# Graph convolution and mixture of experts on one core: bias row by a product, another order of the first loads and of the first projection

## The chip, the cores and the metric

The kernel runs on one core of a Trainium2 chip. The metric is the device time in microseconds of one execution, the median of three runs. Besides these, one execution was recorded by the hardware profiler; its rows are what the text calls the profile or the trace. TensorE multiplies matrices, VectorE (DVE) and ScalarE (ACT) do elementwise work, GpSimd (POOL) makes constants and starts indirect transfers, SyncE (SP) only starts transfers. SP, ACT and POOL each have a queue of transfers of their own; all of them are carried out by the same 16 transfer engines.

## The reference

The input is x (625 rows of 1024), 20000 edges as src and dst (sorted by dst) with a type of 0 or 1, and the weights. Cut to what matters:

```python
h = layernorm(x)
n = ln_weight * h * rsqrt(mean(h**2) + 1e-6)
out = n @ W_root + conv_bias                     # 1024 -> 286
for r in (0, 1):                                 # mean over the edges of one type
    out += segment_sum(n[src] @ W_rel[r] * (type == r), dst) / max(count, 1)
x = x + h + elu(out) @ wo                        # 286 -> 1024
t = layernorm(x)
shared = mean over 2 of gelu(t @ sW1 + sb1) @ sW2 + sb2
gates = t @ rW + rb                              # 8 experts, the two largest, softmax
moe = sum of weight * (gelu(t @ W1[e] + b1[e]) @ W2[e] + b2[e])
result = x + t + shared + moe
```

## The kernel before

All of it is float32 at the edges of each stage; a float32 product shows as two records per product in the trace. The 625 rows are five blocks of 125.

**Edges as a product.** The sums over edges are not gathered. The kernel counts, for every pair of a source and a destination row and for each type, how many edges there are, and multiplies this count matrix with the projected rows. It holds the edges in 160 columns of 125. `edge_columns` (L664) turns the three integer rows into columns: VectorE converts (L667, L670, L672), TensorE transposes (L677, `p_edge`), ACT and VectorE write the half-precision keys `cols` (L687 to L695). For each group of 4 or 8 columns VectorE builds one-hot matrices (`ohs`, `ohk`; three instructions at L849, L850, L852), and TensorE multiplies them into the counts (`cnt`, L868). `count_out` (L811) unpacks finished counts.

**Normalization and transposes.** `stats(t)` (L753) takes mean and variance of block t on VectorE and subtracts the mean on ACT (L765), giving `h`. `to_columns` (L789) transposes h on TensorE (`p_t`, L795, eight per block); ACT evicts the first four with the layer-norm weight as a scale (L801), VectorE the other four (L798). `scales` (L771) works out the two reciprocal roots.

**Projections.** `project(i)` (L886) multiplies one block by one of the three weight matrices: sixteen records of 286 columns (`p_pr`, L891). Projections 0 to 4 are with W_root and are evicted with their scale and the bias `cb` (L901); 5 to 9 and 10 to 14 are with the two W_rel and are split into three bfloat16 parts (L895 to L899). `aggregate(d, r)` (L904) multiplies counts and parts (`p_agg`), takes the edge count of each row from the last column (`deg`, copied by ACT at L911) and adds the mean (L913 to L915). `elu`, `elu_columns` and `output_proj` (L920 to L966) finish the convolution, store the rows and normalize again (`h2`), and `to_columns` brings h2 into `h2T`.

**Experts.** `gate` (L1078) multiplies with the gate weights, `route` (L1102) finds the two largest, `slots` (L1150) gives each pair of row and expert a place in one of eleven tiles. The first layer of the two shared experts, `shared_in` (L1132, `p_sh`), is placed between these steps, so that TensorE works while VectorE routes. Then eleven tiles of gathered rows go through the experts (L1359, L1417), and the second layer of the shared experts is added last (L1472).

**What sets the order.** The code writes an order by hand: `at(c, f, ...)` says that f comes behind the counts of edge column c (L984 to L1021). In front of the loop stand the steps

```python
warm(24)                  # L975: products of constants, only to keep TensorE at work
behind = edge_columns()
transpose_lnw()
warm(40)
ahead = stats(0)
```

`tc.issue_after(x.ins)` says that an instruction stands behind another one in its engine's order. Within these bounds a planner sets each engine's order at build time: it takes by the code's order what it holds to be ready, so that, for example, a projection can be cut in two with counts between. On the chip, each engine then goes through its list in this order. The first loads are issued by SP in this order: edge types, src, x's block 0, W_root, x's blocks 1, 2 and 3 (one transfer), 4, the two W_rel. ACT's queue issues dst and the layer-norm weight. POOL's queue issues the convolution bias, read 125 times into `cb` (L610), then biases and gate weights. Accumulators in PSUM are taken from two rings, `ps_acc` (three slots in the first half) and `ps_mm` (three).

Of the kernel before, what the change touches and what calls it, by code (L numbers as in the profile page):

```python
# [8 lines left out]
F32 = mybir.dt.float32  # L9
# [3 lines left out]
I16 = mybir.dt.int16  # L13
# [439 lines left out]
def sparse_kernel(  # L453
# [68 lines left out]
    for name, v, eng in (("ety", edge_type, nc.sync), ("dst", dst, nc.scalar), ("src", src, nc.sync)):  # L522
        ti = fbig.tile([EH, 2 * EP], I32, name=f"{name}_i")
        eng.dma_start(ti, v.rearrange("(c p) -> c p", p=2 * EP))
        rows_i[name] = ti
# [5 lines left out]
    nc.scalar.dma_start(lnw, ln_w.rearrange("(k p) -> k p", p=128))  # L531

# [9 lines left out]
    def load_w(r, w):  # L542
        nc.sync.dma_start(wg[:, :, r, :], w.rearrange("(k p) f -> p k f", p=128))

    load_x(0, 1)
    load_w(R, W_root)
    load_x(1, 1)
    load_x(2, 2)
# [61 lines left out]
    nc.gpsimd.dma_start(cb, bcast_rows(conv_bias, TP))  # L610
# [53 lines left out]
    def edge_columns():  # L664
# [7 lines left out]
        nc.vector.tensor_copy(rowf[:, 0], rows_i["src"])  # L672
        p = ps_mm("p_edge")
        pv = p[:EP, : 2 * EC].rearrange("p (a j c) -> p a j c", a=2, j=2)
        for a in (0, 1):
            for j in range(2):
                nc.tensor.transpose(pv[:, a, j, :], rowf[:, a, j * EP : (j + 1) * EP], ident[:EH, :EH])  # L677
        wide = [EP, EH, 2, 2]

        def column(v):  # L680
            return v.rearrange("p (c j) b -> p c j b", j=2)

        def pairs(v):
            return v.rearrange("p j c -> p c j")[:, :, :, None].to_broadcast(wide)

        with tc.issue_after(table.ins):
            nc.scalar.copy(column(cols[:, KW_]), pairs(pv[:, 1]))  # L687

        q = fbig.tile([EP, 3, 2, EH], F32, name="q")
        nc.vector.tensor_scalar(q[:, 0], pv[:, 0], -float(TP // 2), 1.0 / TP, op0=ALU.add, op1=ALU.mult)  # L690
        nc.vector.tensor_scalar(q[:, 1], q[:, 0], ROUND, -ROUND, op0=ALU.add, op1=ALU.add)
        nc.vector.scalar_tensor_tensor(q[:, 2], q[:, 1], -float(TP), pv[:, 0], op0=ALU.mult, op1=ALU.add)
        nc.scalar.copy(column(cols[:, SP_]), pairs(q[:, 2]))

        return nc.vector.tensor_scalar(column(cols[:, VV_].bitcast(I16)), pairs(q[:, 1]), 4096.0, 7168.0,  # L695
                                       op0=ALU.mult, op1=ALU.add)
# [39 lines left out]
    def transpose_lnw():  # L736
        p = ps_mm("p_lnw")
        nc.tensor.transpose(p[:, :KD], lnw, ident[:KD, :KD])
        nc.scalar.copy(lT, p[:, :KD])

# [12 lines left out]
    def stats(t):  # L753
        st = small.tile([TP, 2, 6], F32, tag="st", name=f"st_{t}")
        for s in range(2):
            with tc.issue_after((second[0] if t > 1 else evicted[1] if t else behind).ins):
# [4 lines left out]
        h = rows.tile([TP, D], F32, tag="h", name=f"h_{t}")  # L761
        with ExitStack() as order:
            if t == 1:
                order.enter_context(tc.issue_after(evicted[0].ins))
            moved = nc.scalar.activation(h, xh[:TP, t, :], AF.Identity, bias=neg)  # L765
# [61 lines left out]

    def count_windows(between):
        accs = []
        c0 = 0  # L830
        for g in GROUPS:
            oh_s = oneh.tile([EP, MAXG, 128], F16, tag="oh_s", name=f"ohs_{c0}")
            oh_k = oneh.tile([EP, MAXG, KR], F16, tag="oh_k", name=f"ohk_{c0}")

            def both(what, n):
                return [EP, g, n // 2, 2], cols[:, what, c0 : c0 + g][:, :, None, :].to_broadcast([EP, g, n // 2, 2])

            def halves(v):
                return v.rearrange("p g (a b) -> p g a b", b=2)

            order = ExitStack()
            if c0 == 0:
                order.enter_context(tc.issue_after(ahead.ins))
            elif c0 == 8:
                order.enter_context(tc.issue_after(second[0].ins))
            row = iota[:EP].rearrange("p (a b) -> p a b", b=2)
            shape, key = both(SP_, 128)
            os = halves(oh_s[:, :g, :])
            nc.vector.tensor_tensor(os, row[:, None].to_broadcast(shape), key, op=ALU.is_equal)  # L849
            nc.vector.tensor_tensor(os, os, both(VV_, 128)[1], op=ALU.mult)  # L850
            shape, key = both(KW_, KR)
            nc.vector.tensor_tensor(halves(oh_k[:, :g, :]), row[:, None, :SPAN].to_broadcast(shape), key,  # L852
                                    op=ALU.is_equal)
            order.close()
# [49 lines left out]
    def aggregate(d, r):  # L904
# [6 lines left out]
        nc.scalar.copy(deg[:, R * d + r : R * d + r + 1], p[:TP, F : F + 1])  # L911
        inv = small.tile([TP, 2], F32, tag="inv", name=f"inv_{d}_{r}")
        nc.vector.tensor_scalar(inv[:, 0:1], p[:TP, F : F + 1], 1.0, None, op0=ALU.max)  # L913
# [61 lines left out]
    warm(24)  # L975
    behind = edge_columns()
    transpose_lnw()
    warm(40)
    ahead = stats(0)
# [7 lines left out]
    for t, (c0, c1) in enumerate(((0, 3), (4, 9), (13, 19), (16, 22), (20, 26))):  # L987
        if t:
            at(c0, stats, t)
        at(c1, to_columns, t, None, nT, True)  # L990
# [11 lines left out]
    at(6, scales, 0, 2)  # L1002
    at(18, scales, 2, 4)
    at(21, scales, 4, NT)
    for i, c in enumerate((7, 15, 21, 24, 28, 46, 64, 82, 100, 118, 134, 148)):
        at(c, project, i)
# [21 lines left out]

    count_windows(between)
# [13 lines left out]
    load_w1(range(2))  # L1043
    sh_in = ExitStack()
# [478 lines left out]
```

## Time and profile before

| what | value |
|---|---|
| median of three runs | 304.66 us (304.27 to 304.80) |
| the profiled execution, its own time | 303.7 us |
| its span, first to last instruction | 301.4 us |
| instructions | 4682 |
| mean granted TensorE clock | 0.997 |
| read from HBM, written | 42.76 MB, 18.81 MB |
| x's block 0, W_root: last packet ends | 5.61 us, 10.42 us |
| first projection (`p_pr`) starts | 11.79 us |
| first shared product (`p_sh`) starts, rank product starts | 130.04 us, 143.27 us |
| last product ends | 296.2 us |

The profile's rows give, for a group of instructions, the engine, the line, the operation, what it writes and reads, the count, and the time. Times are from the span's start. PEld is the loading of weights, which runs beside the products. In the chain of waits each piece was released by the one before it or stood behind it on its engine; a wait names the engine that waits, the engine it waits for, the total, the number of times and the longest one.

### The profile page before, as it was taken

Reading aid. Unit: us, or ns where it says so; the run is one execution under the profiler, and the core shown is the slowest. Engines: PE = TensorE matmul, PEld = TensorE weight load, DVE = VectorE, ACT = ScalarE, POOL = GpSimd, SP = SyncE. Lnnn points to the kernel's source line nnn. Section 1 sums busy time; section 2 is a strip of 40 time slices with the busy share of each in tenths; the row PEclk is TensorE's granted clock in tenths of the full one; section 3 lists DMA queues with packets and bytes.
Section 4 is the critical chain, followed back from the end, with each engine's and each line's share of the span. In section 5 each row is a group of like instructions: output and inputs, shape, how many; then the busy total and the mean of one; then the engine's idle time right before and its main releaser. Section 6 shows DMA issues by size and latency. Waiting matters only on the chain.

```text
span 301.4 us, 4682 instructions
## 1 busy us (share of the span) xinstructions
PE 290.8 (96%) x1649; PEld 194.9 (65%) x1649; DVE 168.4 (56%) x465; ACT 107.5 (36%) x246; POOL 45.2 (15%) x98
## 2 busy tenths in 40 slices
PE   8799999999999799999999999999999999999993
PEld 6687777787889534376777887887843334444452
DVE  5999999998327668756883122212223211255921
ACT  2455118355334432155123244638359311000000
POOL 9500000000000014240131212210003222200000
PEclk9999999999999999999999999999999999999998
DMA  7999910000009999965999253340057555479442
GB/s 243 304 318 393 421 65 2 0 2 1 0 17 340 348 348 391 400 195 182 348 396 410 86 203 96 114 141 3 0 190 276 221 209 210 191 291 385 161 138 73
DMA packets 27408, 61.15 MB, mean 203 GB/s; under 512 B 2176, under 2 KB 16007, under 8 KB 27375
## 3 DMA queue, kind: packets, MB, share of 16 engines
q1 hardware_dynamic: 21806, 43.77, 40.7%
q0 software_dynamic: 5280, 16.69, 15.7%
q10 hardware_dynamic: 294, 0.35, 0.5%
q8 instruction: 15, 0.25, 0.3%
q14 instruction: 13, 0.10, 0.1%
HBM read 42.76 MB, written 18.81 MB: 204 GB/s over the span
## 4 chain that ended last, share of the span: by engine, by line
PE 93%; DVE 4%; ACT 1%; issue 0%; ACTq 0%
PE p_pr L891 20%; PE p_h L1359 13%; PE p_yj L1417 13%; PE p_o L1472 11%; PE p_sh L1137 10%; PE p_y L952 6%; PE p_agg L909 6%; PE p_x L1340 3%; PE p_t L795 3%; PE cnt L868 2%; PE p_y L956 2%; PE p_hT L1371 1%; PE scrap L972 1%; PE p_gate L1085 1%; PE p_o L1474 1%; DVE ln_4s L727 0%
## 5 line engine op out<-in xcount | busy, mean ns | idle before, releaser
L891 PE MATMUL p_pr<-wg,nT 128*125 128x286 f32 x240 | 62.5, 409 | 0.0
L891 PEld LDWEIGHTS p_pr<-wg,nT 128*125 128x125 f32 x240 | 43.2, 187 | 11.3 <-ACT nT L801 0.2
L1359 PE MATMUL p_h<-w1a,xsT 128*128 (+2 forms) x176 | 40.0, 380 | 0.0
L1417 PE MATMUL p_yj<-w2a,hjT 128*128 (+2 forms) x88 | 38.6, 594 | 0.0
L1472 PE MATMUL p_o<-sw,shT 128*125 128x512 f32 (+1 forms) x88 | 36.1, 553 | 0.0
L1137 PE MATMUL p_sh<-h2T,sw 128*128 128x313 f32 (+1 forms) x128 | 35.2, 428 | 0.0
L1359 PEld LDWEIGHTS p_h<-w1a,xsT 128*128 128x128 f32 (+2 forms) x176 | 28.7, 168 | 7.4 <-issue 0.5
L1137 PEld LDWEIGHTS p_sh<-h2T,sw 128*128 128x128 f32 x128 | 23.6, 189 | 8.6 <-issue 0.2
L1417 PEld LDWEIGHTS p_yj<-w2a,hjT 128*128 128x128 f32 (+2 forms) x88 | 14.4, 168 | 22.4 <-issue 22.4
L1472 PEld LDWEIGHTS p_o<-sw,shT 128*125 128x125 f32 x88 | 16.4, 187 | 16.9 <-issue 16.2
L1421 DVE COPY ys<-p_yj 128x512 f32<-128x512 f32 x15 | 10.4, 692 | 28.7 <-PE p_yj L1417 26.5
L1363 DVE COPY hj<-p_h 128x256 f32<-128x256 f32 x11 | 4.7, 425 | 30.8 <-PE p_h L1359 30.8
L909 PE MATMUL p_agg<-P,CT 125*125 125x287 bf16 x150 | 20.1, 287 | 1.6 <-DVE agg L915 1.6
L966 POOL DMA_DIRECT2D x1d<-xh x10 | 5.3, 532 | 98.5 <-DVE xh L959 98.5
L909 PEld LDWEIGHTS <-CT 125*125 125x125 bf16 x150 | 18.5, 136 | 2.5 <-issue 2.0
L1425 POOL DMA_INDIRECT yt<-ys,row x11 | 10.8, 984 | 50.5 <-DVE ys L1421 50.5
L952 PE MATMUL p_y<-wo_t,eT 128*125 128x512 f32 x40 | 18.1, 595 | 0.0
L1332 POOL DMA_INDIRECT xs<-h2d,tok x11 | 11.2, 1015 | 45.0 <-PE p_x L1340 30.9
L1374 ACT ACTIVATE hjT<-p_hT,vT 128x128 f32<-128x128 f32 (+2 forms) x34 | 8.7, 332 | 24.5 <-PE p_hT L1371 24.5
L1344 DVE COPY xsT<-p_x 128x512 f32<-128x512 f32 x11 | 7.6, 692 | 17.4 <-PE p_x L1340 13.8
L1448 DVE SCALAR_TENSOR_TENSOR x<-p_o,x 125x512 f32<-125x512 f32 (+1 forms) x11 | 6.9, 641 | 16.3 <-PE p_o L1474 16.3
L1359 PE MATMUL p_h<-w1m,xsT 128*64 128x256 f32 (+1 forms) x96 | 14.7, 381 | 0.0
(302 smaller groups left out, 424.0 us busy)
## 6 DMA issues: line engine op xcount, KB each, us to landing
w1a<-in_L_ffn_W_dram SPq DMA_DIRECT2D x8, 1024.0 KB, 10.5
w2a<-in_L_ffn_W_dram SPq DMA_DIRECT2D x8, 1024.0 KB, 4.8
yt<-zero SPq DMA_DIRECT2D x2, 2560.0 KB
g<-yt SPq DMA_DIRECT2D x10, 512.0 KB, 6.7
sw<-in_L_ffn_sW_dram SPq DMA_DIRECT2D x4, 1024.0 KB, 5.0
x<-x1d SPq DMA_DIRECT2D x5, 500.0 KB
wg<-in_L_gnn_W_rel_dram SPq DMA_DIRECT2D x2, 1144.0 KB, 19.1
x1d<-xh POOLq DMA_DIRECT2D x5, 448.0 KB, 6.7
```

The costliest lines, as they stand in the source:

```text
L795: nc.tensor.transpose(pv[:, k, :], row[:, at : at + 128], ident[:TP, :TP])
L891: nc.tensor.matmul(p[:TP, :F], nT[:, k, m * TP : (m + 1) * TP], wg[:, k, r, :], start=(k == 0), stop=(k == KD - 1))
L909: nc.tensor.matmul(p[:TP, : F + 1], CT[:, m, at : at + TP], P[:, m, r, i], start=(m == 0 and i == 0), stop=(m == NT - 1 and i == 2))
L952: nc.tensor.matmul(ps[s][:TP, :], eT[:, k, :], wo_t[:, k, s * 512 : (s + 1) * 512], start=(k == 0), stop=False)
L1137: nc.tensor.matmul(p[:, : z - a], sw1[:, i, k, t * 128 : (t + 1) * 128], h2T[:, k, a:z], start=(k == 0), stop=(k == KD - 1))
L1332: nc.gpsimd.indirect_dma_start(out=xs, out_offset=None, in_=h2d, in_offset=bass.IndirectOffsetOnAxis(ap=tok[:, j : j + 1], axis=0))
L1340: nc.tensor.transpose(p[:, k * 128 : (k + 1) * 128], xs[:, at : at + 128], ident)
L1359: nc.tensor.matmul(p[a:b, :H], xsT[j][:, k, a:b], w1m[j, a][:, 0, k, :] if a else w1a[:, bass.ds(e, 1), k, :], start=(k == 0), stop=(k == ...
L1417: made = nc.tensor.matmul(p[a:b], hjT[:, j, k, a:b], w2m[j, a, k][:, at] if a else w2a[:, bass.ds(e, 1), k, at], start=(k == 0), stop=(k = ...
L1421: nc.vector.tensor_copy(y[:, at], p)
L1425: sent.append(nc.gpsimd.indirect_dma_start(out=yt, out_offset=bass.IndirectOffsetOnAxis(ap=row[:, j : j + 1], axis=0), in_=y, in_offset=No ...
L1472: nc.tensor.matmul(p[:TP, :n], shT[:, i, k, own], sw2[:, i, k, at], start=(i == 0 and k == 0), stop=False)
```

## The change

The convolution bias is loaded as one row by ACT's queue and spread over the 125 rows by a product with a row of ones, in place of the repeated load by POOL's queue. src is issued by ACT's queue. x's block 1 is issued ahead of W_root, and W_root in two halves. The statistics of block 0 stand ahead of the source columns on VectorE, and for blocks 0 and 1 the subtraction of the mean is divided between ACT (384 columns) and VectorE (640). The edge transposes go to two PSUM tiles, and the source keys are written by VectorE alone. The fillers are 18 and 14 in place of 24 and 40. Transposes and projection of block 0 come ahead of all counts; the one-hots of the first four columns are built behind block 0's eviction, and later projections stand some columns earlier. The degrees are copied by VectorE. The first product of the shared experts (sixteen records) is written out ahead of the transposes of the last block, and the other shared products are tied behind the gate's last product and behind the load counts.

```diff
-    for name, v, eng in (("ety", edge_type, nc.sync), ("dst", dst, nc.scalar), ("src", src, nc.sync)):
+    for name, v, eng in (("ety", edge_type, nc.sync), ("dst", dst, nc.scalar), ("src", src, nc.scalar)):
...
+    cb1 = fbig.tile([1, F], F32, name="cb1")
+    nc.scalar.dma_start(cb1, conv_bias.rearrange("(o f) -> o f", o=1))
...
-    def load_w(r, w):
-        nc.sync.dma_start(wg[:, :, r, :], w.rearrange("(k p) f -> p k f", p=128))
+    def load_w(r, w, *ks):
+        for k in ks or (slice(0, KD),):
+            nc.sync.dma_start(wg[:, k, r, :], w.rearrange("(k p) f -> p k f", p=128)[:, k])
     load_x(0, 1)
-    load_w(R, W_root)
     load_x(1, 1)
+    load_w(R, W_root, slice(0, KD // 2), slice(KD // 2, KD))
     load_x(2, 2)
...
     cb = gbig.tile([TP, F], F32, name="cb")
-    nc.gpsimd.dma_start(cb, bcast_rows(conv_bias, TP))
+    one = fbig.tile([1, TP], F32, name="one")
+    nc.vector.memset(one, 1.0)
...
+        ps = [ps_acc("p_edge"), ps_mm("p_edge_k")]
         for a in (0, 1):
             for j in range(2):
-                nc.tensor.transpose(pv[:, a, j, :], rowf[:, a, j * EP : (j + 1) * EP], ident[:EH, :EH])
+                nc.tensor.transpose(ps[a][:EP, j:EC:2], rowf[:, a, j * EP : (j + 1) * EP], ident[:EH, :EH])
...
-        nc.vector.scalar_tensor_tensor(q[:, 2], q[:, 1], -float(TP), pv[:, 0], op0=ALU.mult, op1=ALU.add)
-        nc.scalar.copy(column(cols[:, SP_]), pairs(q[:, 2]))
+        nc.vector.scalar_tensor_tensor(cols[:, SP_], pairs(q[:, 1]), -float(TP), pairs(v),
+                                       op0=ALU.mult, op1=ALU.add)
...
         nc.scalar.copy(lT, p[:, :KD])
+        p = ps_mm("p_cb")
+        nc.tensor.matmul(p[:TP, :F], one, cb1, start=True, stop=True)
+        nc.scalar.copy(cb, p[:TP, :F])
...
-            with tc.issue_after((second[0] if t > 1 else evicted[1] if t else behind).ins):
+            with tc.issue_after((second[0] if t > 1 else first if t else behind).ins):
                 nc.vector.bn_stats(st[:, s, :], xh[:TP, t, s * 512 : (s + 1) * 512])
...
+        own, rest = (slice(0, 384), slice(384, D)) if t < 2 else (slice(0, D), None)
...
-            moved = nc.scalar.activation(h, xh[:TP, t, :], AF.Identity, bias=neg)
+            moved = nc.scalar.activation(h[:, own], xh[:TP, t, own], AF.Identity, bias=neg)
+        if rest:
+            with tc.issue_after(last.ins):
+                last = nc.vector.tensor_scalar(h[:, rest], xh[:TP, t, rest], neg, None, op0=ALU.add)
...
+            if c0 < 8:
+                order.enter_context(tc.issue_after((second[0] if c0 else evicted[1]).ins))
...
-        nc.scalar.copy(deg[:, R * d + r : R * d + r + 1], p[:TP, F : F + 1])
+        n = deg[:, R * d + r : R * d + r + 1]
+        nc.vector.tensor_copy(n, p[:TP, F : F + 1])
         inv = small.tile([TP, 2], F32, tag="inv", name=f"inv_{d}_{r}")
-        nc.vector.tensor_scalar(inv[:, 0:1], p[:TP, F : F + 1], 1.0, None, op0=ALU.max)
+        nc.vector.tensor_scalar(inv[:, 0:1], n, 1.0, None, op0=ALU.max)
...
-    warm(24)
-    behind = edge_columns()
+    warm(18)
+    behind, sources = edge_columns()
     transpose_lnw()
-    warm(40)
-    ahead = stats(0)
+    warm(14)
+    source_columns(sources, stats(0))
+    to_columns(0, hs[0], nT, True)
...
-    for t, (c0, c1) in enumerate(((0, 3), (4, 9), (13, 19), (16, 22), (20, 26))):
+    for t, (c0, c1) in enumerate(((0, 3), (6, 11), (9, 14), (13, 18))):
         if t:
-            at(c0, stats, t)
-        at(c1, to_columns, t, None, nT, True)
+            at(c0, stats, t + 1)
+        at(c1, to_columns, t + 1, None, nT, True)
...
-    at(6, scales, 0, 2)
-    at(18, scales, 2, 4)
-    at(21, scales, 4, NT)
-    for i, c in enumerate((7, 15, 21, 24, 28, 46, 64, 82, 100, 118, 134, 148)):
-        at(c, project, i)
+    at(10, scales, 2, 4)
+    at(14, scales, 4, NT)
+    for i, c in enumerate((3, 12, 15, 20, 38, 56, 74, 92, 110, 128, 146)):
+        at(c, project, i + 1)
...
+    oh_s, oh_k, first = one_hots(0, GROUPS[0])
+    made[0] = oh_s, oh_k
+    stats(1)
+    scales(0, 2)
+    project(0)
     count_windows(between)
...
+        if s == NT + 1:
+
+            p_first = ps_acc("p_sh_first")
+            for k in range(KD):
+                nc.tensor.matmul(p_first[:, : CUTS[0][1]], sw1[:, 0, k, :128], h2T[:, k, : CUTS[0][1]],
+                                 start=(k == 0), stop=(k == KD - 1))
         if 0 <= s - 2 < NT:
             to_columns(s - 2, h2s[s - 2], h2T, False)
...
-        shared_in(0, 0)
+        shared_in(0, 0, gated)
...
-        shared_in(0, 1)
+        shared_in(0, 1, loaded)
```

## The prediction

> **What bounds the kernel now.** I read first the page's busy times and slices, then the chain of waits with the list of what TensorE waits for, then the transfers in half-microsecond windows, then the timeline of the two other places where TensorE stands still.
>
> ```profile
> PE 290.8 (96%) x1649; PEld 194.9 (65%) x1649; DVE 168.4 (56%) x465; ACT 107.5 (36%) x246; POOL 45.2 (15%) x98
> ...
> PE   8799999999999799999999999999999999999993
> ...
> DVE  5999999998327668756883122212223211255921
> ```
>
> TensorE is full from the second slice to the last. VectorE is full too, but only from 7.5 to about 68 us: after that it has room. So time comes only from TensorE's idle places, and VectorE must feed whatever starts earlier.
>
> ```profile
> 5.21 0.88 PE p_edge L677 x4
> ...
> 6.57 0.34 DVE q L690
> ...
> 7.76 1.21 DVE st L757 x2
> ...
> 9.91 0.35 DVE ohs L850
> ...
> 10.62 1.07 PE p_t L795 x8
> 11.70 0.11 PE cnt L868 x4
> 11.81 4.10 PE p_pr L891 x16
> ```
>
> Start, length and work of the chain. What stands before 10.3 us is preparation; the products at L972 are fillers that only keep TensorE busy. From 11.81 on, one piece of product work follows another, so each microsecond by which the first projection (p_pr) starts earlier is a microsecond at the end, if its followers keep up.
>
> ```profile
> PE cnt L868 <- DVE ohs L850: 1.7, 1, 1.7
> PE p_agg L909 <- DVE agg L915: 1.6, 1, 1.6
> ...
> PE p_t L795 <- DVE h L731: 0.6, 1, 0.6
> ```
>
> These are TensorE's waits behind the start: 1.7 (8.6 to 10.3 us), 1.6 (to 100.16) and 0.6 (to 133.47). Nothing else is to be had.
>
> ```profile
> 7.00:7.50 0.50, 0.50 (x12) 0.50 (x10) 0.47 (x3) 0.00 (x0) 0.50 (x2) 1.00 1.91 398
> 7.50:8.00 0.50, 0.50 (x12) 0.50 (x10) 0.50 (x3) 0.44 (x1) 0.48 (x2) 1.00 0.92 121
> 8.00:8.50 0.50, 0.50 (x11) 0.44 (x8) 0.50 (x2) 0.02 (x1) 0.17 (x1) 1.00 1.06 108
> 8.50:9.00 0.50, 0.11 (x3) 0.00 (x0) 0.47 (x2) 0.00 (x0) 0.00 (x0) 1.00 0.53 55
> 9.00:9.50 0.50, 0.00 (x0) 0.00 (x0) 0.47 (x3) 0.08 (x1) 0.00 (x0) 1.00 0.61 206
> ```
>
> The last column is GB/s. Between 7.5 and 9.5 us it falls from about 390 to a mean of 122. The trace's packets tell why: in just this time the bias's 31 broadcast packets of 4576 bytes run at about 0.9 us each, and the packets of W_root, 51 ns each around them, hardly move. W_root's last packet ends at 10.42 us, x's row 0's at 5.61.
>
> **The start, step by step.** *Edge columns.* The fillers ahead fall from 24 to 18. The 24 took 2.74 us, so the edge transposes could start 0.5 us earlier, about 4.5; their last input (the src copy) is ready at 4.22. They end at 5.5. That they go to two banks frees VectorE from waiting for ACT's copy (6.54 today), but it works on row 0 then, so nothing. The memset of ones is 0.06 before any input is there. src moves from SP's queue to ACT's: SP loses 0.41 us of issue ahead of x's row 0, ACT gains 0.41 and, for the bias row, about 0.5; ACT's table load moves from 1.80 to 2.7 and ends at 4.0, before ACT's first copy at 5.5, so nobody sees it.
>
> *Row 0's statistics.* They now stand ahead of the source columns on VectorE, right behind the src copy (4.22), but need x's row 0. Issued 0.46 earlier (1.19 for 1.65), it lands at 5.15, between 4.7 (most of it is there by 4.82 today) and 5.6 (no earlier than today, if src in ACT's queue takes its turns). From 5.15: statistics, mean and negation take 1.65 today (7.76 to 9.39), so 6.8; then h in two parts side by side. VectorE's 640 columns: 1024 take 0.81 at L731 and 286 take 0.30 at L927, so 0.55. ACT's 384 of 1024 (1.15 today): 0.55. h is there at about 7.4, where it is 10.57 today.
>
> *Bias product and fillers.* Two records of 286 columns, 0.5 us on TensorE, and a 0.45 us copy on ACT, at about 6.0 and 6.5: in the wait for h. Then 14 fillers at 0.06 are 0.84, to about 7. The other 18 removed cost nothing. Here the Trainium skill speaks against the change (TensorE: Matmul & The Clock Gate, Part 1): about 3.4 us of sustained work release the full clock. The row: the first 24 fillers take 114 ns each and the later 40 take 60, so the clock comes up between 5.0 and 6.2, with TensorE at work since 1.5. The changed start is as dense up to 7, and today 1.7 us of idling slows nothing (8 transposes in 1.07, as later). By the row the cost is nil; were the release missed, by the rule up to 3.4 us at half speed, 1.7 lost.
>
> *First projection.* Transposes of row 0 from 7.45; today the projection starts 1.17 behind them, so 8.6 in place of 11.79. It no longer waits for the one-hots of the first four edge columns (9.3 to 10.3 today).
>
> *Does W_root arrive?* Row 1 of x (512 KB) now goes ahead of it, 1.4 us at the 375 GB/s of 5 to 7 us. But half of W_root is enough to begin (572 KB, 1.5 us); the second is wanted 2.05 later; the extra issue is 0.43 on SP. Row 0's main part to about 4.4, row 1 to 5.8, first half to 7.4, second to 9; with today's spread between the transfer engines (0.8 for row 0) 8.2 and 9.8, for 8.6 and 10.65. This holds only because the broadcast goes. By the skill's fit (DMA: Bandwidth & Descriptors, Anatomy of one DMA: 2.0 us plus bytes over 436 GB/s) its 143 KB take 0.33 us of bandwidth from others; by the row it is (390 - 122) x 2.0 = 536 KB, 1.4 us. I take the row: by the rule, the second half would still be hit by what the broadcast does. The GpSimd queue behind it (vec, rb, bd, rW) comes 0.8 to 3 us earlier, since bd's 2.3 us wait for the broadcast goes too; the slow stretch at 13.75 to 15 (229 GB/s for 410, some 0.5 us) then falls on x's later rows, which landed 2 us before they were used.
>
> **What follows behind.** VectorE: source columns 1.3 (ACT's 0.46 copy becomes part of one of its four operations) to 8.65; row 0's eviction 0.65 to 9.3; one-hots of the first four columns 0.7 to 10.0; row 1's statistics and h 2.2 to about 12.3. The projection ends at 12.7, so row 1's transposes start at 12.8 and projection 1 at 14.0, in place of 16.89: 2.9, as no counts are left to fill the 0.2 between. VectorE gains 2.6 by starting its long run at 5.1 instead of 7.7, and pays 1.3 for the source columns and 1.1 for two parts of h. It is thus only about 0.2 earlier while TensorE is 2.9 earlier. The counts in the program stand 8 columns (1.75 us of one-hots) later at each projection, so 1 us is missing; today it is ahead by ten to eighteen columns at 37 us, 2 to 4 us. Later TensorE takes counts as they come (counts at 53.68 behind one-hots that end at 53.62), with projections between them, and 15 us of projection and aggregation remain after the last count at 73.1. That cover is shortened by 3 and holds. Front: 3.0 (from 2.5 to 3.5).
>
> **Aggregation.** ACT's degree copy goes (0.16, x10), VectorE's comes (0.15). At the 1.6 us wait, ACT copied late (98.61, behind an exponential) and VectorE stood 0.35 for it. Bounds: 0.5 gained if the copy goes first, 0.1 lost if it stands behind L928. I take 0.2; elsewhere 0.15 lies beside products.
>
> **Shared experts.** Today ten of the sixteen records of the first product fill the gap before row 4's transposes and 0.63 us stays idle; two pairs of records fill the gate's gaps.
>
> ```profile
> 130.04 2.80 PE L1137 MATMUL p_sh<-h2T,sw 128*128 128x313 f32 x10
> 133.47 1.04 PE L795 MATMUL p_t<-ident,h 125*128 125x125 f32 x8 [0.63 <-DVE h L731]
> 134.44 1.92 PE L1085 MATMUL p_gate<-h2T,rw_t 128*32 128x125 f32 x64
> 136.29 0.80 PE L1137 MATMUL p_sh<-h2T,sw 128*128 128x313 f32 x2
> ```
>
> All sixteen (at 0.266: 4.27) now go first, to 134.3, so the transposes start 0.84 later but meet no idle time. The rest waits for the gate's last product. From 130.04 to the rank product at 143.43 are 13.39; work is 32 x 0.266 + 1.00 + 1.84 + 0.56 + 0.44 = 12.36. Left over in future: TensorE behind the gate's second VectorE copy (0.35 and two handovers, less a 0.30 transpose), about 0.2, and 0.15 of changes. Gain 0.7, from 0.3 (the second pair of gaps opens fully) to 0.9. The routing takes VectorE 2.95 from the gate's last product, under the 4.27 of the sixteen records behind it. Tying the next shared product behind the load counts moves nothing: it stands there today.
>
> **Sum.** 3.0 + 0.2 + 0.7 = 3.9. The profiled execution took 303.7 (span 301.4, 2.3 around it), so 299.8; the median is 304.66, 0.96 above it, so 300.8. A difference within 0.2% can't be told from none here.
>
> **Rivals.** *The forecast*, 66%: 299.8 to 301.8. *VectorE takes over in part*, 12%: row 1's h or the later one-hots come about 1.5 late; for it: 98% busy from 10 to 60 us; against: today's lead. 302.3. *Row 1 delays W_root*, 7%: if the slow stretch comes from other small transfers, the first half lands at 10.4 as W_root does today, 1.8 gone: 302.6. *The clock stays down*, 3%: 302.5. *The order isn't what it says*, 5%: if the planner puts the first projection behind the counts again, only the two later parts are left and the time is 303.8 to 304.5. *Slower*, 7%: the last projections stand behind the last count in TensorE's order. If they are held there, TensorE goes at the pace of VectorE's one-hots, which end at 72.1 today. VectorE's run has 2.4 us more in it and pauses for evictions; should row 0 land at 5.6 and two pauses of 1.0 come, the last one-hot is 1.6 late and the whole front with it: 304.66 + 1.6 - 0.9 = 305.4. This decides from the point where the one-hots end more than 0.9 later than now.
>
> Range 299.6 to 303.0: the first four cases but their edges. Faster 0.89, same 0.04, slower 0.07, out of the same cases.
>
> **What would show it.** First projection at 8.6, second near 14.0; the rate at 7.5 to 9.5 us near 380; W_root's halves before 8.6 and 10.6; no count waiting for one-hots between 15 and 73 us; no idle time ahead of row 4's last transposes and the rank product 0.7 closer behind the first shared product. Wrong if the first projection starts at 10 or later, or TensorE shows new waits of over 1 us for one-hots.

## The result and the profile after

The changed kernel takes 306.28 us (median of five runs, 306.10 to 306.96), the kernel before 304.49 us beside it (304.27 to 304.80): a ratio of 1.006, with an interval of 1.0045 to 1.0075. It is slower by 0.6%, clear of the noise, and the forecast was 300.8. The profiled execution of the changed kernel took 306.33 us with a span of 304.1; that of the kernel before 303.7 and 301.4.

TensorE's places in the two traces divide the difference; the forecast's column is worked out from its own terms (its 3.0 in front and 0.2 in the aggregation together move the first `p_y`).

| stretch on TensorE, us | before | forecast | after |
|---|---|---|---|
| start to first projection (`p_pr`) | 11.79 | 8.60 | 11.91 |
| first projection to first `p_y` | 90.85 | 90.85 | 93.17 |
| first `p_y` to first shared product | 27.40 | 27.40 | 27.39 |
| first shared product to rank product | 13.23 | 12.53 | 13.28 |
| rank product to the end of the last product | 152.95 | 152.95 | 152.95 |
| from there to the end of the span | 5.23 | 5.23 | 5.43 |

So 3.3 us are missing at the start, 2.3 up to the first `p_y`, 0.75 in the middle. The timeline of TensorE in the start of the changed kernel (start, length, work; in brackets the idle time ahead and what ended it):

```profile
2.59 2.10 PE L988 MATMUL scrap<-iota 128*128 128x128 f16 x18
6.40 0.68 PE L680 MATMUL p_edge<-ident,rowf 80*125 80x80 f32 x2 [1.71 <-DVE rowf L676]
6.87 0.62 PE L680 MATMUL p_edge_k<-ident,rowf 80*125 80x80 f32 x2
7.42 0.27 PE L741 MATMUL p_lnw<-ident,lnw 8*128 8x8 f32 x1
7.55 1.29 PE L744 MATMUL p_cb<-cb,one 1*125 1x286 f32 x2
8.77 1.67 PE L988 MATMUL scrap<-iota 128*128 128x128 f16 x14
10.24 1.87 PE L806 MATMUL p_t<-ident,h 125*128 125x125 f32 x8
11.91 4.57 PE L906 MATMUL p_pr<-wg,nT 128*125 128x286 f32 x16
```

Two things are to be seen. There is a hole of 1.71 us ahead of the edge transposes. And every row is long: a filler takes 119 ns in the second group too, the transposes 1.87 (1.07 before), the projection 4.57 (4.12 before). In the kernel before the second group ran at 60 ns each:

```profile
6.21 2.41 PE L972 MATMUL scrap<-iota 128*128 128x128 f16 x40
```

In the trace's own clock record the full clock begins at 12.98 us; in the kernel before it began at 6.22. The profile's clock column shows 1.00 for the start in either case, so it can't be used here: the record holds nothing ahead of its first entry, and only the durations show that TensorE ran at half speed until then. h of block 0 is written by 8.53 us; its transposes stand behind slow fillers until 10.24.

The chain of waits begins with the cause of the hole:

```profile
1.20 4.67 DMA src_i<-in_src_dram
```

src, now in ACT's queue, lands at 5.36 us (last packet); in SP's queue, ahead of x's rows, it landed at 3.03. Clock entries and packets are counted here from the span's start, like the instructions. The table of the kernel before, the prediction and the expectations count them from 0.24 us earlier: the table's 5.61 and 10.42 us are 5.37 and 10.18. The list of TensorE's waits has one new entry in the front and two in the middle, and the one at `p_agg` (1.6 before) is where it was:

```profile
PE p_agg L924 <- DVE agg L931: 1.5, 1, 1.5
PE p_gate L1112 <- DVE gT L1115: 0.6, 1, 0.6
PE p_t L806 <- ACT h L773: 0.4, 1, 0.4
PE p_gr L1119 <- DVE gT L1115: 0.2, 1, 0.2
```

What the bias product was meant for did happen. The rate (last column, GB/s) no longer falls at 7.5 us:

```profile
7.50:8.00 0.50, 0.50 (x2) 0.50 (x3) 0.43 (x3) 0.47 (x3) 0.50 (x2) 1.00 1.09 374
8.00:8.50 0.50, 0.50 (x2) 0.02 (x1) 0.50 (x2) 0.50 (x2) 0.50 (x1) 1.00 1.09 349
```

W_root's first half lands at 8.47 us and the second at 10.22, row 0 of x at 5.68 (8.2, 9.8 and 5.15 in the forecast, by its count). The weights were there; the work was not ready for them.

### The profile page after: what moved, and what is told of

The parts are those of the page before. It is cut to its first block, busy times and chain, and to the rows that moved or that the text cites. A ratio compares the mean times of both kernels' runs of the same rounds, so it can differ in the third digit from the quotient of the medians.

```text
span 304.1 us, 4626 instructions
## 1 busy us (share of the span) xinstructions
PE 292.3 (96%) x1619; PEld 194.6 (64%) x1619; DVE 171.1 (56%) x478; ACT 104.9 (35%) x236; POOL 44.5 (15%) x97
## 4 chain that ended last, share of the span: by engine, by line
PE 90%; DVE 5%; DMA 2%; ACT 1%; issue 1%; ACTq 0%; DVEq 0%
PE p_pr L906 17%; PE p_h L1391 13%; PE p_yj L1449 13%; PE p_o L1504 11%; PE p_sh L1169 10%; PE p_y L968 6%; PE p_agg L924 4%; PE p_x L1372 3%; PE p_t L806 3%; PE p_y L972 2%; DMA src_i<-in_src_dram 2%; PE cnt L883 1%; PE p_sh_first L1089 1%; DVE ct L827 1%; PE p_hT L1403 1%; PE p_gate L1112 1%
## 5 line engine op out<-in xcount | busy, mean ns | idle before, releaser
L906 PE MATMUL p_pr<-wg,nT 128*125 128x286 f32 x240 | 64.0, 413 | 0.1
L1169 PE MATMUL p_sh<-h2T,sw 128*128 128x312 f32 (+1 forms) x112 | 30.4, 428 | 0.0
L1169 PEld LDWEIGHTS p_sh<-h2T,sw 128*128 128x128 f32 x112 | 20.9, 189 | 7.7
L1364 POOL DMA_INDIRECT xs<-h2d,tok x11 | 10.6, 961 | 45.8 <-PE p_x L1372 30.9
```

What stands on the lines that cost most here:

```text
L906: nc.tensor.matmul(p[:TP, :F], nT[:, k, m * TP : (m + 1) * TP], wg[:, k, r, :], start=(k == 0), stop=(k == KD - 1))
L1169: nc.tensor.matmul(p[:, : z - a], sw1[:, i, k, t * 128 : (t + 1) * 128], h2T[:, k, a:z], start=(k == 0), stop=(k == KD - 1))
L1364: nc.gpsimd.indirect_dma_start(out=xs, out_offset=None, in_=h2d, in_offset=bass.IndirectOffsetOnAxis(ap=tok[:, j : j + 1], axis=0))
```

## The experiments

Theory A: src's late landing and a late clock hold up the start. Theory B: VectorE has become the bound, and the start hardly matters. Theory C: the middle part takes back what it gives. Times of one batch stand beside runs of the kernel before on the same chip, whose medians were 305.49, 304.98, 304.52 and 304.78 us in the four batches. Single times of one kernel there spread over 2.6 to 3.7 us, so the positions in the traces carry most of the argument. These are the runs, with the time from which the clock record has the full clock:

| run | fillers ahead of the edge transposes | full clock from | fillers behind, ns each | first projection | first `p_y` |
|---|---|---|---|---|---|
| before | 24 | 6.22 | 60 | 11.79 | 102.64 |
| before once more (e8) | 24 | 5.96 | 60 | 11.79 | 103.67 |
| before, src on ACT (e3) | 24, then 0.88 idle | 11.55 | 110 | 12.90 | 103.75 |
| before, bias by product (e4) | 24, then that product | 10.51 | 96 | 12.41 | 103.27 |
| before, 18 fillers (e9) | 18 | 10.57 | 111 | 11.45 | 102.53 |
| after | 18, then 1.71 idle | 12.98 | 119 | 11.91 | 105.08 |
| after, src on SP (e1) | 18 | 10.31 | 120 | 10.37 | 103.33 |
| e1, bias product later (e5) | 18 | 15.50 | 119 | 11.47 | 104.99 |
| after, 34 fillers (e2) | 34 | 6.05 | 68 | 10.14 | 102.85 |
| after, both mended (e6) | 34 | 5.72 | 68 | 9.91 | 102.90 |

**e1: src back in SP's queue.**

```diff
-("src", src, nc.scalar)
+("src", src, nc.sync)
```

> The changed kernel with src issued by SP ahead of x's row 0 again; all else stays. Theory A (the late src is the whole cause): src's last packet ends near 3.3 us instead of 5.6, the edge transposes start at 4.7 instead of 6.4, TensorE has no 1.7 us hole there, its fillers behind run at 60 ns instead of 119, the first projection starts near 9.0 instead of 11.91, the sixth (first with a W_rel) near 35.8 instead of 38.65, and the time is 303.4 or less. Rival B (VectorE's longer list in front of the first projections is a bound of its own): the first projection comes to about 9.0 all the same, but the sixth only to 37 or so, and the time stays at 304 to 305. Rival C (x's row 0, not src, sets the start): the first projection stays above 10.5.

304.72 us, ratio 0.998 [0.996, 1.0001], span 302.4. src lands at 3.00, the edge transposes start at 4.62 and the hole is gone; the first projection comes 1.54 earlier, at 10.37 and not near 9.0 as theory A had it. The fillers stayed slow:

```profile
4.62 0.68 PE L680 MATMUL p_edge<-ident,rowf 80*125 80x80 f32 x2
6.99 1.68 PE L988 MATMUL scrap<-iota 128*128 128x128 f16 x14
```

The clock came only at 10.31, though TensorE had next to no idle time from 1.6 us on (0.03). The late src is a cause, not the only one.

**e2: 34 fillers in front, src left on ACT.**

```diff
-    warm(18)
+    warm(34)
```

> The changed kernel with 34 fillers instead of 18 ahead of the edge transposes, so that TensorE has work until src is there; src stays late. Theory A with the clock as its larger part: the edge transposes start at 6.5 as before the edit, but the bias product takes about 0.5 instead of 1.29, the 14 fillers about 0.85 instead of 1.67, the eight transposes 1.07 instead of 1.87; the first projection starts near 9.8 instead of 11.91 and the time falls by about 2. If the clock played no part and only the late src did: first projection within 0.3 of 11.9, time within 0.5 of the changed kernel's.

304.74 us, ratio 0.9982 [0.9945, 1.0018], span 302.2. This alone brings 1.9 us of span back:

```profile
2.59 3.71 PE L988 MATMUL scrap<-iota 128*128 128x128 f16 x34
6.48 0.41 PE L680 MATMUL p_edge<-ident,rowf 80*125 80x80 f32 x2 [0.18 <-DVE rowf L676]
```

The edge transposes are as late as in the changed kernel, but take 0.41 in place of 0.68, and all that follows is at full speed.

**e3 and e4: one part of the change, put into the kernel before.** e3 moves src to ACT's queue. e4 spreads the bias by the product.

> The kernel before with one edit: src issued by ACT's queue instead of SP's. Theory A: src's last packet ends past 5 us instead of at 3.3, since x's row 0 and W_root fill the same transfer engines from SP's queue; the edge transposes start near 6.0 instead of 4.9, the first projection about 1 later than 11.79, and the time is 0.8 to 1.5 above the kernel before. Rival (the late src comes from something else in the change, such as row 1 of x ahead of W_root): src lands before 4 us and the time is within 0.3 of the kernel before.

> The kernel before with one edit: the bias row spread by a product instead of loaded 125 times. Both theories: the rate between 7.5 and 9.5 us rises from a mean of 122 GB/s to over 300, W_root's last packet ends near 8.8 us instead of 10.42; since the first projection starts at 11.79 for other reasons, the time stays within 0.4 of the kernel before. A gain of 1 us or more would mean that W_root had been a bound.

e3: 305.82 us, ratio 1.0009 [0.9985, 1.0034], span 303.1; src lands at 4.87, the first projection is 1.1 later. e4: 304.79 us, ratio 0.9989 [0.9972, 1.0006], span 302.3; W_root lands at 8.79 for 10.18 and the slump is gone (398 GB/s from 7.5 to 9.5 us for 123), which the first projection does not use, since it waits for VectorE's one-hots; it comes 0.6 later, by the clock. Both parts, harmless in the prediction, delay the clock, by 5.3 and 4.3 us, in a kernel whose fillers were sufficient.

**e5: the bias product behind block 0's transposes** (src on SP), to see whether this product of a single row is what keeps the clock down.

```diff
-        p = ps_mm("p_cb")            # in transpose_lnw
+    spread_bias(to_columns(0, hs[0], nT, True))   # tied behind the last transpose
```

> The changed kernel with src back in SP's queue and the bias product moved behind block 0's eight transposes, where TensorE waits for the evictions. Theory 1 (the bias product, 286 columns of work on a single row, is what keeps the clock down in the start): the clock is full by 6.3 to 7.5 us, fillers behind the edge transposes at 60 ns, the first projection at 8.7 to 9.3 in place of 10.37 with the product in its old place, span 301.0 (302.4 less 1.4). Theory 2 (the time of the release is not set by what TensorE does in this start, it differs from run to run): it comes anywhere between 6 and 13 us, and the first projection with it.

306.32 us, ratio 1.0047 [1.0028, 1.0067], span 304.4. The theory fell: without the product in the start the clock came later still, at 15.50, and the first projection took 6.10 us. What the mended starts have and this one lacks is the longer run of fillers.

**e6, e7: 34 fillers and src on SP; e7 also frees the shared product.**

```diff
-        shared_in(0, 0, gated)
+        shared_in(0, 0)
```

> The changed kernel with src in SP's queue and 34 fillers in front for 18. Theory 1 (unbroken dense fillers release the clock, as with 34 fillers and late src at 6.29): full clock at 6.3, edge transposes at 5.5, first projection at 9.2 to 9.6, span 301.6, about 0.6 less than with late src (302.2), since the fillers themselves now reach to 5.4. Theory 2 (release not set by the work): anything from 6 to 13 us, first projection up to 11. Theory 3 (VectorE sets the later projections): whatever the first projection gains, projection 3 waits again for VectorE's or ACT's h, and the sixth projection starts no earlier than 36.2.

> As the kernel with both mended, but the second half of the first shared product is no longer tied behind the gate's last product, so records of it can fill the gate's gaps. Theory (the tie took as much as the first product ahead of the transposes gave): from the first shared product to the rank product 12.6 to 12.8 us in place of 13.28, the 0.6 us wait of p_gate for gT gone, span 0.5 less than with the tie. Rival (the gaps come from VectorE's chain whatever stands in them): 13.2 or more.

e6: 303.64 us, ratio 0.9979 [0.9948, 1.0009], span 301.6. First projection at 9.91, 1.88 ahead of the kernel before; the first `p_y`, at 102.90, is 2.2 ahead of the changed kernel's and not ahead of the kernel before at all. So theory A explains the start, which does matter, and some 2 us are lost behind it (1.9 in e7). Of the expectation's theories, the first has the clock right and the first projection a little early, and the third fits: the sixth projection starts at 36.48. e7: 304.9 us, ratio 0.9994 [0.9969, 1.0018], span 301.2. Its gate waits are gone, but from the first shared product to the rank product it still takes 13.25. The gap has only moved, as TensorE's line shows, and then VectorE's timeline why:

```profile
143.29 0.23 PE L1189 MATMUL p_rank<-sel,below 125*125 125x40 f16 x1 [0.67 <-DVE sel L1143]
```

```profile
141.76 0.91 DVE L637 MEMSET b2x<- 96x1024 f32 x1 [0.16 <-issue]
142.59 0.42 DVE L1142 TENSOR_REDUCE cnt<-above 125x40 f32<-125x320 f32 x1
143.05 0.18 DVE L1143 TENSOR_SCALAR sel<-cnt 125x40 f16<-125x40 f32 x1
```

A memset of 0.91 us for a later stage stands ahead of `cnt` and `sel` in VectorE's order. In the kernel before it stood behind `sel`:

```profile
141.39 0.18 DVE L1115 TENSOR_SCALAR sel<-cnt 125x40 f16<-125x40 f32 x1
141.73 0.91 DVE L633 MEMSET b2x<- 96x1024 f32 x1 [0.15 <-DVE sel L1115]
```

The planner moved it; no line of the diff mentions it. It stands ahead of `sel` in the changed kernel too, but there the tie has already delayed TensorE, so that `sel` is ready in time.

**e8: the kernel before once more.**

> The kernel before, unchanged, once more. Theory 1 (work sets the release of the clock): full clock at 6.3 to 6.6 us again and the first projection at 11.8. Theory 2 (it differs from run to run): full clock at another time, up to 3 us away; the fillers behind the edge transposes then take over 100 ns.

304.92 us, ratio 1.0001 [0.9978, 1.0025]. The clock and the first projection come again about where they did (5.96 and 11.79). But the first `p_y` is 1.03 later, and the span 303.3 for 301.4. One of VectorE's waits, which the first profile does not have, is about as long:

```profile
DVE st L757 <- DMA xh<-in_x_dram: 0.9, 2, 0.8
```

In this run W_root landed at 11.23 for 10.18, and x's rows behind it came late for the statistics. e12 and e13, with the same loads, show this wait too (2.2 and 0.4); the first profile and e9 do not. So the first profile, from which the forecast was worked out, was a lucky one. In all five the packets of the bias's broadcast end only just ahead of W_root's (9.7 to 10.7 us). That the broadcast is what makes the rows late in some executions is likely, and not shown.

**e9: the kernel before with 18 fillers for 24.**

> The kernel before with 18 fillers ahead of the edge transposes for 24 and nothing else. Theory (the clock's release needs a stretch of about 3.4 us that dense fillers fill; with 18 they end at 4.6 and every such stretch holds the edge transposes or a hole): the clock is not full at 6.5 us but at 9 to 13, the 40 fillers behind take over 100 ns each, the first projection starts at 12.3 to 13.5 in place of 11.79, span 302.3 to 303.5. Rival (the two sorts of start differ for another reason): full clock at 6.3 to 6.6, first projection at 11.8 or up to 0.4 earlier, span 301.0 to 301.5.

304.8 us, ratio 1.0002 [0.9978, 1.0027], span 301.3. The clock came at 10.57, as the theory said, and the first projection at 11.45, which it had not said:

```profile
5.62 4.45 PE L972 MATMUL scrap<-iota 128*128 128x128 f16 x40
9.87 0.40 PE L868 MATMUL cnt<-ohk,ohs 125*128 125x58 f16 x4
```

Forty fillers at 111 ns just fill the wait for the one-hots. In the old order a late clock is hidden by that wait; in the changed order the wait is removed, and with it the cover.

**e10: VectorE's memset tied behind `sel`** (on e7).

```diff
-        nc.vector.memset(b2x, 0.0)
+        with tc.issue_after(chosen.ins):      # chosen: the instruction that writes sel
+            nc.vector.memset(b2x, 0.0)
```

> As the kernel with both mended and the shared product untied, but VectorE's memset of 0.91 us (b2x) is put behind the instruction that writes sel, ahead of which it stands in the changed kernel's order of VectorE (in the kernel before it stands behind). Theory (this memset took what the middle part should give): the wait of p_rank for sel (0.7 us) goes, the first shared product to the rank product takes 12.6 us in place of 13.25, span about 300.6. Rival (the second wait of 0.1 to 0.3 comes from elsewhere, p_load then waits): 12.9 to 13.2.

303.72 us, ratio 0.9974 [0.9951, 0.9996], span 301.0: faster than the kernel before, just clear of the noise. VectorE's order, then TensorE's rank product:

```profile
142.40 0.18 DVE L1144 TENSOR_SCALAR sel<-cnt 125x40 f16<-125x40 f32 x1
142.74 0.91 DVE L638 MEMSET b2x<- 96x1024 f32 x1 [0.15 <-DVE sel L1144]
```

```profile
142.69 0.18 PE L1191 MATMUL p_rank<-sel,below 125*125 125x40 f16 x1
```

From the first shared product (130.28) that is 12.41 us, without a wait: 0.84 less. Theory C holds, in two steps, the tie and the memset.

**e11, e12: less work for VectorE.** The multiplication of the one-hots with their value is left out for all but the first four columns; e11 on e7, e12 on the kernel before. The counts are then wrong, and behind them the kernel takes a far longer way (1254.63 and 1256.96 us in all), so only the part up to the first `p_y` is read.

```diff
-        last = nc.vector.tensor_tensor(os, os, both(VV_, 128)[1], op=ALU.mult)
+        last = evicted[1]
+        if c0 < 4:
+            last = nc.vector.tensor_tensor(os, os, both(VV_, 128)[1], op=ALU.mult)
```

> As the kernel with both mended and the shared product untied, but VectorE's multiplication of the one-hots with their value is left out for all but the first four edge columns, so that the counts are not the reference's; VectorE has some 20 us less to do between 10 and 73 us, TensorE's products are the same. Theory (VectorE's one-hots come too late to fill TensorE's gaps between a block's transposes and its projection, and so cut the projections in pieces): from the first projection to the first p_y 90.5 to 91.2 us in place of 92.75, the projections whole, no wait for h. Rival (the order of the projections or ACT's evictions cost it): 92.5 or more.

> The kernel before with the same multiplication left out, so that the counts are not the reference's: the control. Theory (in the kernel before VectorE's pace costs TensorE next to nothing): from the first projection to the first p_y 90.3 to 90.9 us, 90.85 with the multiplication, span at most 0.5 less. Rival (VectorE sets the pace there too): 89.5 or less, span over 1 us less.

e11: from the first projection to `p_y` 90.85 us for 92.75, within the forecast. TensorE's work between is cut into 48 pieces, in e7 into 73 and in the kernel before into 62; the fifteen projections stand in 15, 27 and 20 of them. e12: 92.59 us, outside its forecast. But VectorE waited 2.2 us for x's rows in it, and TensorE stood idle for 2.0 more than in the kernel before; without that 90.6 are left, which was expected. As a control it is weak, since the planner also ordered each of the two anew; in e12 too the fifteen projections are whole.

**e13: the middle part alone, on the kernel before** (first shared product ahead of the last transposes, nothing tied, memset behind `sel`).

> The kernel before with only the middle part: the first shared product ahead of the last transposes, the other shared products untied, and VectorE's memset of b2x behind sel. Theory (the middle part gives 0.8 once nothing is tied and the memset is out of the way, whatever the start does): from the first shared product to the rank product 12.4 us in place of 13.23, the positions ahead of it as in the kernel before, time 0.8 us (0.27%) below it. Rival (the gain of the middle came only with the changed front): 12.9 or more, no difference in time.

304.06 us, ratio 0.9979 [0.9963, 0.9995], span 301.3. From the first shared product (130.62) to the rank product (143.03) it takes 12.41 us, so the middle is worth 0.82 by itself. This execution, too, lost time to a late row of x.

**e14: the mean of blocks 0 and 1 subtracted by ACT alone** (on e10).

> As the kernel with the shared product untied and the memset behind sel, but ACT subtracts the mean of blocks 0 and 1 alone, as in the kernel before; VectorE has about 1.1 us less to do, the first projection can start up to 0.6 us later. Theory (behind the first projection VectorE's pace decides): the first projection starts 0.3 to 0.6 later, at 10.4 to 10.7, but the first p_y starts no later than now (102.89) and up to 0.6 earlier, so from the first projection to p_y 91.6 to 92.4. Rival (TensorE's own order costs the 1.9 us): 92.6 again, and p_y 0.3 to 0.6 later.

303.44 us, ratio 0.9963 [0.9942, 0.9985], span 301.1. The first projection starts at 10.35, but the first `p_y` at 103.42, so 93.07: the theory's figures missed, and the rival's `p_y` (0.3 to 0.6 later) came true. ACT's h became the late one (TensorE waits 0.9 for it, 0.3 in e10), and the clock came only at 7.45. So it does not tell VectorE's pace from the order, and it does not speak for VectorE. Its time is no worse than e10's; the intervals overlap.

**e15: the degrees copied by ACT** (on e10).

> As the kernel with the shared product untied and the memset behind sel, but the degrees are copied by ACT, as in the kernel before. Theory (the copy on VectorE gains nothing): first p_y within 0.2 us of 102.89, TensorE's wait for agg 1.5 to 1.6 us. The prediction's step (0.2 gained by VectorE's copy at that wait): the wait is 1.7 and p_y 0.2 or more later.

304.17 us, ratio 0.9973 [0.9952, 0.9994], span 301.6. TensorE's wait for agg is 1.54 (1.47), `p_y` at 102.85 (102.89), both as the theory said. But e15's first projection started 0.23 later than e10's, at 10.30, so the stretch from there to `p_y` took 92.55 for 92.82. The copy on VectorE thus costs about 0.3. The aggregation agrees: counted from the start of each record to the next, its products take 18.8 us in all eight traces with ACT's copy (18.9 in e12) and 19.0 to 19.1 in all nine with VectorE's. The times of e10 and e15 do not show it, since their intervals overlap.

## Why the prediction was wrong

*src in ACT's queue* (the copy "ready at 4.22", the edge transposes at "about 4.5"). This step failed. The move was priced by issue time alone, and the mention of turns was used only for x's row 0. src's 1000-byte packets in ACT's queue took from 2.72 to 5.36 us beside x's rows: 30 GB/s of the 272 that all queues moved in that time. The Trainium skill (DMA: Bandwidth & Descriptors, Queues, rings and completion order) says that a transfer engine goes round the queues that have work, packet by packet (a packet there holds several of the trace's pieces). If each queue got equal numbers of the trace's pieces of 1000 and 4096 bytes, src would have a fifth of the rate, which at the prediction's 375 GB/s is an estimate of 1.1 us; the trace says 2.6, so the turns were not equal by these pieces. The estimate would already have put the edge transposes a little behind 4.5 (2.7 + 1.1, then 0.5 to VectorE's start and 0.3 for the copy make 4.6); measured, they start at 6.40. Cost: the first projection 1.5 later (e1).

*The clock* ("By the row the cost is nil"; 3% for the rival). This step failed too. The row that I used showed that 24 fillers, the transposes and 40 more were sufficient, not that 18 and 14 are. In the runs, all profiles with 34 fillers have the full clock from between 5.3 and 7.5 us, all with 18 from 10.3 or later. With 24 it is 6.0 to 7.4, unless a hole (e3) or the bias product (e4) follows. The rule that the prediction cites asks for about 3.4 us of sustained work: from the first product to the end of 18 fillers are 3.1, of 24 3.7, of 34 4.3 to 4.8. So the rule spoke against the change. The traces agree with it only in part: 3.7 us were not always sufficient, and in e1 TensorE was busy for 8.7 us before it got the full clock. In all seventeen traces the first stretch of full clock lasts 286.7, 290.1 or 293.5 us; these are 84, 85 and 86 times 3.413, so the clock seems to be granted by windows of that length. Where they begin differs from run to run. Which share of work a window must have stays open: e9 in the 3.4 us up to 7.16 and e13 in those up to 6.96 hold about equal work (2.2 us of fillers, 1.0 of edge transposes), and only e13 had its clock then. The rival's price, 1.7, was about right (e2 gained 1.9 of span); its chance was not.

*Row 0's statistics.* Even with both mended the first projection stands at 9.9, not 8.6. VectorE's statistics start at 6.00 in e7, 0.85 later than said: the last packet of x's row 0 ended at 5.68, and VectorE went on 0.32 later. The forecast let it start with the last packet; this term it put at nothing. The landing was too early as well: in the changed kernel, with its earlier issue, the packet ended at 5.68 too, which is 5.92 by the forecast's count and outside its 4.7 to 5.6. The first profile's 5.37 was an early one; in five executions of the kernel before with the same loads it was 5.4 to 5.9. The other 0.4 was forecast as free: the second tile of the edge transposes (`p_edge_k`) comes from the ring of three that block 0's transposes use too, so these wait until ACT has copied the destination keys out of it, and ACT now does h first (the idle 0.73 ahead of `p_t` in e7, put down to ACT's cols; h is written at 8.37, the copy ends at 8.69, `p_t` starts at 8.73).

*"That cover is shortened by 3 and holds."* It did not. The prediction compared where VectorE's one-hots end with where TensorE needs them last, and not what they do on the way. Today counts fill each gap between a block's transposes and its projection. In e7 TensorE is 1.9 us earlier, but VectorE's first one-hot is 1.2 later, since it stands behind block 0's eviction (e7, then before):

```profile
10.51 0.41 DVE L857 TENSOR_TENSOR ohs<-iota,cols 125x512 f16<-125x512 f16 x1
```

```profile
9.31 0.42 DVE L849 TENSOR_TENSOR ohs<-iota,cols 125x512 f16<-125x512 f16 x1
```

So the counts aren't there, and the gaps stay open:

```profile
20.52 1.23 PE L906 MATMUL p_pr<-wg,nT 128*125 128x286 f32 x4 [0.23 <-ACT nT L812]
...
26.53 0.54 PE L806 MATMUL p_t<-ident,h 125*128 125x125 f32 x3 [0.29 <-ACT h L773]
```

Against the kernel before, e7's transposes, with the idle time behind them, take 0.84 more up to `p_y`, the projections, in smaller pieces, 0.78, the aggregation 0.31; the rest nearly cancels. That is the 1.9. By place, about half of it (0.9) is lost before 30 us, in these gaps; 0.2 from 30 to 50; 0.4 from 70 to 80, where the last counts stand; 0.1 behind; and 0.2 are eight count products that stood ahead of the first projection and now stand behind it. With VectorE's work cut down the stretch is back at 90.85 (e11). The rival "VectorE takes over in part" had 12% and 1.5 us; its price was near, its chance too small. In the changed kernel itself 0.45 more comes from the first projection at half clock. The point that the slower rival named, one-hots that end over 0.9 later, was passed: they end at 75.5 us for 72.2 (in e7, with the start mended, at 73.1, just at that point). The smaller part of the loss lies there.

How much of the 1.9 is VectorE's pace, and how much the planner's new order, stays open. Only e11 speaks for VectorE's pace, and its order is another one too; e12 and e14 do not settle it. 0.3 of the 1.9 are the degree copies (e15). And the 1.9 is counted against the first profile, the lucky one: with late rows the kernel before took 91.88 (e8) and 91.44 (e13) for the stretch that takes e7 92.75, so against those the loss is 0.9 and 1.3.

*Aggregation, 0.2.* The degree copy on VectorE takes 0.07 off this one wait (1.48 for 1.55) and costs about 0.3 beside the other products (e15). The forecast took the latter as free ("elsewhere 0.15 lies beside products").

*Shared experts, 0.7.* The mechanism was right and is worth 0.82 (e13), but not as the change has it. I priced the tie behind the gate at 0.2 (it opened 0.57 and 0.16), and took VectorE's routing at its old 2.95 us; with the memset ahead of `sel` it is 3.85. The rank product of the kernel before was also read as 143.43; its row says 143.27, so 0.87 us was free in this stretch and not 1.03.

*Right were* the slump, its cause and its size (with the broadcast alone gone, e4's W_root landed 1.39 earlier: 1.4 by the prediction's row, 0.33 by the fit that it set beside it), W_root's first half, the unchanged rest, and that the load counts' tie moves nothing (152.95 from the rank product to the last one in both).

## What to carry to other kernels

A wait that is removed was also a cover: list what hid under it (here a late clock, counts that fill gaps) before the gain is booked. Fillers on TensorE are to be priced by how long they run without a break, not by the idle time that they fill; a small transfer that is needed first did better ahead of the large ones in their queue than beside them in another (e1). Where a planner orders the instructions, compare each engine's order before and after: an unrelated memset was enough to keep back the whole gain of the middle part when the tie was gone (e7, e10).

## What the runs showed of the hardware

The first full clock lasted whole multiples of 3.413 us in all seventeen traces, and a busy TensorE did not suffice to get it: e1 had next to no idle time from 1.6 us on and ran at half speed until 10.31. A 78 KB transfer of 1000-byte packets beside 4096-byte packets of another queue landed 1.8 (e3) to 2.3 us later than ahead of them. With the broadcast read of 143 KB, W_root landed between 10.2 and 11.5 us in five executions of the same loads; with the product in its place, and x's row 1 ahead of W_root, it was 10.1 to 10.6 in ten.
